# Block 2's shifts in two batches, its second pass's keys laid out early, the range verdict by a matmul, and two sets of norm statistics moved ahead

## The chip, the cores and the metric

The kernel runs on one NeuronCore of a Trainium2 chip. The metric is device time in microseconds, as the median of several runs. The profile is one execution, recorded by the hardware profiler. The engines are named PE (TensorE, matmuls and transposes), PEld (its weight loads), DVE (VectorE), ACT (ScalarE), POOL (GpSimd) and SP (SyncE, which here only issues DMAs). Each engine takes its instructions in the order in which they were written out for it, and waits on semaphores.

## The reference

Four blocks of a transformer are applied to `x`, 4 batches of 1024 tokens of width 288, with 16 heads of 18. Blocks 0 and 3 are attention over the tokens, attention over a context of 64, and a feed-forward part, all with 8-bit quantised linear layers. Block 1 is a context attention in two parts. Block 2, where most of the change lies, quantises queries, keys, values and probabilities with one scale for the whole tensor:

```python
        q = _fake_quant(q, NBITS)
        k = _fake_quant(k, NBITS)
        v = _fake_quant(v, NBITS)
        scale = 1.0 / np.sqrt(HD).astype(np.float32)
        scores = jnp.einsum('bhqd,bhkd->bhqk', q, k) * scale
        probs = jax.nn.softmax(scores, axis=-1)
        probs = _fake_quant(probs, SMBITS, always_zero=True)   # delta = max(probs) / 255
        out = jnp.einsum('bhqk,bhkd->bhqd', probs, v)
    ...
    n1 = _ln(h, ln1_g, ln1_b)
    h = h + _quant_attention(n1, n1, Wq1, Wk1, Wv1, Wo1, bo1)
    n2 = _ln(h, ln2_g, ln2_b)
    h = h + _quant_attention(n2, encoder_hidden_states, Wq2, Wk2, Wv2, Wo2, bo2)
    n3 = _ln(h, ln3_g, ln3_b)
    proj = n3 @ Wff1 + bff1
    a, gate = jnp.split(proj, 2, axis=-1)
    h = h + a * jax.nn.gelu(gate, approximate=False) @ Wff2 + bff2
```

The scale of the probabilities is the maximum over all batches, heads, queries and keys. So it is known only when every row of scores has been seen once.

## The kernel before

`x` stays in on-chip memory, as 32 tiles of 128 tokens (`NT` = 32, `NTB` = 8 tiles a batch). The blocks run one after the other: 0 and 1 together, then 2, then 3.

**Block 2, self-attention** (`fq_attn`, `fq_passes`). A first pass goes over all scores, four heads and 128 queries at a time: PE multiplies (line 3276), ACT takes the exponential and its row sum (line 2923), DVE the row maximum (line 2930). It leaves `top` and `sums`, 128 x 32 x 16 each: one column for each token tile and head, 512 in all. `prob_shift` (line 2382) turns them into the scale `pd` and a shift per row: reciprocal of the sums, a check of its range (`watch_range`), maximum over all partitions by an all-reduce on POOL, then Ln, Exp and a correction on ACT and DVE. The shift is split into three bfloat16 parts. `add_shift` (line 2405) lays a tile's three parts into the unused columns of a padded tile `spad` (POOL, line 2410), turns it with four transposes on PE (line 2416) and adds it to the queries (DVE, line 2417). With the shift in the queries, the exponential of the second pass gives the probability in steps of `pd`, which only has to be rounded.

The second pass (`attend_levels`, lines 3316 to 3328) goes over batch, half of the queries (4 tiles), head group and key tile. Its keys lie in `kz`, two buffers with zeros between the heads, cleared once by POOL (line 3023) and filled by four DMAs for each head group (`spread`, line 3031). The shifts of the next half, the output product and the queries of the context part are worked off beside it, one step per key tile (`aside`).

**Block 2's tail** (`fq_tail`) does context attention in the same manner (a first pass, `prob_shift`, then `probs` with `add_shift`) and the feed-forward part (`forward`), two generators woven together. Beside it `self_aside` prepares block 3's weights.

**Blocks 0 and 3.** `quant_self` does self-attention batch by batch and `levels(b)` starts with the norm statistics of batch `b` (`norm_stats`, line 1365, all on DVE). The context and feed-forward parts are generators (`ctx_stage`, `ff_stage`) which `run_stages` (line 1240) writes out in an order that a small planner finds: a generator yields what its last step costs on which engine, such as `"d8.5"` for 8.5 us of DVE, and may go on when that time is over.

**Order.** The program text gives each instruction's priority; the framework's scheduler works out the final order of each engine ahead of the run, and may draw an instruction forward past its place in the text when its inputs and its memory are there. Memory of a closed pool is given to later tiles, which then wait for the last use of what lay there.

**The verdict.** Each `watch_range` writes a column of `bad`. At the end `verdict` (line 1196) takes its maximum, over the columns on DVE and over the partitions by an all-reduce on POOL (line 1202); all engines load the result and branch: where a range was left, everything is computed again in a general way.

Of the kernel before, what the change touches and what calls it, by code (L numbers as in the profile page):

```python
# [21 lines left out]

# [33 lines left out]
class Net:  # L56
# [773 lines left out]
    def log_shift(self, pool, nm, sums, d, name):  # L830

        nc = self.nc
        n = sums.shape[1]
        y = pool.tile([P, n], F32, name=f"{name}y")
        nc.vector.tensor_scalar(y, sums, d, None, ALU.mult)
        z = pool.tile([P, n], F32, name=f"{name}z")
        nc.scalar.activation(z, y, AF.Ln)
        nc.vector.tensor_tensor(nm, nm, z, ALU.subtract)

        nc.scalar.activation(z, z, AF.Exp, scale=-1.0)  # L840
        nc.vector.tensor_tensor(z, z, y, ALU.mult)
        nc.vector.tensor_scalar(z, z, -1.0, 1.0, ALU.mult, ALU.add)
        nc.vector.tensor_tensor(nm, nm, z, ALU.add)
# [335 lines left out]
class Fast(Net):  # L1179
# [6 lines left out]
    def __init__(self, ctx, tc):  # L1186
        super().__init__(ctx, tc)
        self.bad = self.cp.tile([P, 96], F32, name="bad")
        self.n_bad = 0
        self.nmagic = self.cp.tile([P, 1], F32, name="nmagic")  # L1190
        self.nc.vector.memset(self.nmagic, -MAGIC)
        self.tiny = self.cp.tile([P, 1], F32, name="tiny")
        self.nc.vector.memset(self.tiny, 1e-8)
        self.nc.vector.memset(self.bad, 0.0)

    def verdict(self):

        nc = self.nc
        s = self.cp.tile([P, 1], F32, name="bads")
        nc.vector.tensor_reduce(s, self.bad, AX.X, ALU.max)  # L1200
        al = self.cp.tile([P, 1], F32, name="bada")
        nc.gpsimd.partition_all_reduce(al, s, P, bass_isa.ReduceOp.max)
        fl = self.cp.tile([1, 1], mybir.dt.int32, name="badi")
        nc.vector.tensor_copy(fl, al[0:1, :])
        return nc.values_load(fl[0:1, 0:1])
# [569 lines left out]
    def quant_self(self, L, w, beside, ready):  # L1775
# [5 lines left out]
        with ExitStack() as es:  # L1781
# [36 lines left out]
            def levels(b):  # L1818
# [5 lines left out]
                stats = self.norm_stats(b, 1e-6)  # L1824
# [169 lines left out]
            for b in range(B):  # L1994
                state[b]["a"] = at.tile([P, NTB, C], F32, tag="a", name="a")
                for g in range(NG):
                    if g + 1 < NG:
                        side.insert(0, operands(b, g + 1))
                    elif b + 1 < B:
                        while side:  # L2000
                            step()
                        side.append(operands(b + 1, 0))
                    if g == 1 and b + 1 < B:
# [145 lines left out]
    def ctx_stage(self, cw, g2, b2, pool, nb):  # L2149
# [15 lines left out]
        def tokens(b, hf):  # L2165
            t0 = b * NTB + hf * 4
            if hf == 0:
                stats[b] = self.norm_stats(b, 1e-5)
                there[b] = yield "d8.5", None, SIDE
# [212 lines left out]
    def prob_shift(self, gp, tp, top, sums, step):  # L2382


        nc = self.nc
# [5 lines left out]
        self.watch_range(self.R_MIN, self.R_MAX, r, "wr")  # L2391
        u = flat(top)
        nc.vector.tensor_tensor(r, r, u, ALU.mult)
        pd = self.prob_params(gp, r, "pd")
        nc.vector.memset(u, 0.0)
        self.log_shift(tp, u, flat(sums), pd, "ls")
        nc.vector.tensor_scalar(u, u, rstep, None, ALU.mult)
        parts = gp.tile([P, 3, NT * H], BF16, name="parts")
        for k in range(3):
            nc.vector.tensor_copy(parts[:, k, :], u)  # L2400
            if k < 2:
                nc.vector.tensor_tensor(u, u, parts[:, k, :], ALU.subtract)
        return pd, parts

    def add_shift(self, qT, sp, parts, t):


        nc = self.nc
        for k in range(3):
            nc.gpsimd.tensor_copy(  # L2410
                sp[:, :, D + k : D + k + 1], parts[:, k, t * H : (t + 1) * H].unsqueeze(2)
# [433 lines left out]
    def fq_passes(self, w, q, step, raw, rawq, qmx, qmn, side, aside):  # L2845

        tc, nc = self.tc, self.nc
        with ExitStack() as es:
# [8 lines left out]

            tops = ExitStack()
# [74 lines left out]
            with tops:  # L2933
                pd, parts = self.prob_shift(gp, tp, top, sums, step)
            es.enter_context(self.psum("f1o"))

# [3 lines left out]
            at, ot, ep = pool("f1o", 1), pool("f1q", 2), pool("f1p", 2)  # L2940
# [4 lines left out]
            spad = at.tile([P, H, HP], BF16, name="spad")  # L2945
            nc.gpsimd.memset(spad, 0.0)

            def shifts(b, hf):
                for j in range(hf * 4, hf * 4 + 4):
                    t = b * NTB + j  # L2950
                    self.add_shift(qk[:, b, 0, :, j * P : (j + 1) * P], spad, parts, t)
                    yield
# [68 lines left out]
            kzs = [at.tile([P, 2, S], BF16, name=f"kz{n}") for n in range(2)]  # L3021
            for kz in kzs:
                nc.gpsimd.memset(kz, 0.0)

            def spread(n):

                kz = kzs[n % 2]
                b, g = n // (2 * NG), n % NG
                for i in range(4):
                    rows = slice(i * HP, (i + 1) * HP)  # L3030
                    nc.sync.dma_start(kz[rows, i % 2, :], qk[rows, b, 1, g, :])

            spread(0)
            side.append(shifts(0, 0))
            while side:
                aside()
            late = []
            for b in range(B):
                for qh in range(2):
                    side[:0] = [shifts(*divmod(2 * b + qh + 1, 2))] if 2 * b + qh + 1 < 2 * B else []  # L3040
# [17 lines left out]
    def fq_tail(self, w, kq, keep, rawq, mx, nmn, beside):  # L3058
# [5 lines left out]
        with ExitStack() as es:  # L3064
# [6 lines left out]
            with (  # L3071
# [62 lines left out]
                pd, parts = self.prob_shift(gp, qp, top, sums, step)  # L3134
# [125 lines left out]
            for _ in spare:  # L3260
                pass
            self.weave([forward(before)], 1, 1)
# [178 lines left out]
```

## Time and profile before

| what | us |
|---|---|
| runs | 5096.9, 5111.57, 5107.95; median 5107.95 |
| the profiled execution | 5098.57 |
| its span, first to last instruction | 5096.9 |
| block 2, first pass (end of the scale's parameters to its last maximum) | about 1812 to 2414 |
| block 2, between the passes | 2414 to 2442 |
| block 2, second pass | 2442 to about 2990 |
| block 2, tail | from about 3004 |
| block 3, context and feed-forward parts | about 4640 to 5080 |

Over the whole span PE is busy 86%, ACT 61%, DVE 58% and POOL 26%; the granted clock of TensorE is 0.84 in the mean.

A line of the timeline gives start and duration in us, the engine (a q after it means its queue, which issues), the line of the code, the operation, what it writes and reads with the shape, how many instructions are merged, and in brackets how long the engine had been idle and which instruction ended that. A busy time by stretches gives the same for a stretch of time in one row.

### The profile page before, as it was taken

The numbers are of one execution on the slowest core, as the hardware profiler recorded it, in microseconds if no ns is written. First come the engines' busy times: TensorE is split into PE (matmuls) and PEld (weight loads), VectorE is DVE, ScalarE is ACT, GpSimd is POOL, SyncE is SP. The second block draws the span as 40 slices with busy tenths as digits, with TensorE's granted clock in tenths as the row PEclk, the third lists the DMA queues.
The fourth block names the chain that finished last, engine by engine and source line by source line (L and its number), as shares of the span: only waits on it lengthen the run. The fifth ranks groups of instructions, "written<-read, shape, count | busy, mean of one in ns | idle before, by whom it ended". The sixth has DMA issues, their size and how long they took to land. (4 is left out here: it accounts for less than half of the span.)

```text
span 5096.9 us, 63943 instructions
## 1 busy us (share of the span) xinstructions
PE 4360.7 (86%) x23291; PEld 1742.5 (34%) x23291; DVE 2961.5 (58%) x6542; ACT 3128.5 (61%) x4422; POOL 1348.8 (26%) x2109
## 2 busy tenths in 40 slices
PE   5999997889898979998788863899998999996686
PEld 2223322545565421100233332454542223322343
DVE  7343244665564679999687877433234334344775
ACT  3766765466663259998788853212216766764796
POOL 2110002442422566200122234111103110003664
PEclk9999998899899965555787875899998999997897
DMA  2000002100001221000000032000000000010000
GB/s 78 3 4 12 5 26 61 57 23 16 1 12 38 114 82 39 11 0 0 23 27 25 25 105 79 21 10 10 1 7 9 7 2 11 15 25 30 16 17 20
DMA packets 135637, 135.99 MB, mean 27 GB/s; under 512 B 69260, under 2 KB 111884, under 8 KB 133648
## 3 DMA queue, kind: packets, MB, share of 16 engines
q1 hardware_dynamic: 134112, 128.13, 8.4%
q0 software_dynamic: 1200, 3.69, 0.3%
q8 instruction: 185, 3.03, 0.2%
q14 instruction: 140, 1.15, 0.1%
HBM read 79.92 MB, written 43.47 MB: 24 GB/s over the span
## 5 line engine op out<-in xcount | busy, mean ns | idle before, releaser
L2021 ACT ACTIVATE e<-ps 128x1024 f32<-128x1024 f32 x1024 | 997.5, 1021 | 450.1 <-PE ps L2011 439.7
L2011 PE MATMUL ps<-qT,kT 32*128 32x512 f32 x4096 | 699.1, 658 | 1.8 <-ACT e L2021 1.8
L1971 PE MATMUL ps<-e,v 128*32 128x512 f32 x4096 | 564.1, 621 | 22.8 <-DVE oT L1982 21.1
L2930 DVE TENSOR_REDUCE top<-e 128x2 f32<-128x2048 f32 x256 | 561.9, 2275 | 18.5 <-ACT e L2923 18.5
L2923 ACT ACTIVATE e<-ps 128x1024 f32<-128x1024 f32 x512 | 534.0, 1369 | 19.7 <-PE ps L3276 11.3
L3325 ACT ACTIVATE e<-ps 128x1024 f32<-128x1024 f32 x512 | 484.0, 1056 | 84.3 <-PE ps L3316 67.3
L3276 PE MATMUL ps<-qk 32*128 32x512 bf16 x1024 | 511.1, 604 | 24.6 <-ACT e L2923 23.4
L1758 POOL TENSOR_TENSOR x<-x,y 128x288 f32<-128x288 f32 x192 | 153.1, 808 | 873.3 <-DVE y L1757 529.0
L1404 POOL TENSOR_TENSOR h<-h,g 128x288 f32<-128x288 f32 x224 | 179.5, 805 | 701.3 <-ACT h L1401 663.5
L3328 DVE TENSOR_SCALAR eb<-e 128x2048 bf16<-128x2048 f32 x256 | 322.0, 1261 | 48.6 <-ACT e L3325 46.1
L2923 ACT ACTIVATION_READ_ACCUMULATOR e<-ps 128x1 f32 x512 | 280.6, 550 | 0.0
L2011 PEld LDWEIGHTS ps<-qT,kT 32*128 32x128 f32 x4096 | 201.9, 187 | 226.0 <-issue 144.7
L3316 PE MATMUL ps<-qk,kz 64*128 64x512 bf16 x1024 | 225.0, 437 | 45.6 <-ACT e L3325 43.6
L2454 PE MATMUL psf<-hT,w 128*128 128x512 f32 x576 | 258.2, 600 | 0.6 <-ACT hT L2446 0.6
L1971 PEld LDWEIGHTS ps<-e,v 128*32 128x32 f32 x4096 | 81.9, 109 | 427.6 <-issue 353.6
L1349 PE MATMUL ps<-idb,q 128*128 128x128 bf16 (+2 forms) x1152 | 112.9, 243 | 124.5 <-ACT q L1333 70.8
L1401 ACT ACTIVATE h<-x,nmr,rstd 128x288 f32<-128x288 f32 x224 | 129.4, 623 | 137.7 <-DVE nmr L1393 69.7
L3276 PEld LDWEIGHTS <-qk 32*128 32x128 bf16 x1024 | 52.7, 99 | 465.4 <-issue 465.4
L3225 ACT ACTIVATE gl<-psf,bf 128x512 f32<-128x512 f32 x72 | 46.0, 684 | 268.5 <-PE psf L2458 264.2
L1354 ACT COPY qT<-ps 98x384 bf16<-98x384 bf16 (+3 forms) x256 | 151.6, 642 | 75.8 <-PE ps L1349 75.7
L1405 POOL TENSOR_TENSOR h<-h,b 128x288 f32<-128x288 f32 x224 | 180.4, 808 | 4.5
L277 PEld LDWEIGHTS <-qT 98*128 98x128 bf16 (+2 forms) x1344 | 135.7, 105 | 129.0 <-issue 43.9
(484 smaller groups left out, 7633.0 us busy)
## 6 DMA issues: line engine op xcount, KB each, us to landing
raw<-y SPq DMA_DIRECT2D x32, 432.0 KB
in<-raw SPq DMA_DIRECT2D x32, 432.0 KB
kz<-qk SPq DMA_DIRECT2D x128, 64.0 KB
wn<-in_L_wfc SPq DMA_DIRECT2D x12, 432.0 KB
x<-in_x SPq DMA_DIRECT2D x4, 1152.0 KB
vvo<-vt SPq DMA_DIRECT2D x16, 288.0 KB
vo<-vvo SPq DMA_DIRECT2D x4, 1152.0 KB
rawq<-y SPq DMA_DIRECT2D x32, 144.0 KB
```

Source lines behind the costliest of these rows:

```text
L1404: nc.gpsimd.tensor_tensor(h, h, g, ALU.mult)
L1405: nc.gpsimd.tensor_tensor(h, h, beta, ALU.add)
L1971: nc.tensor.matmul(acc[i * HP : (i + 1) * HP, :], lhsT=st["v"][:, kt, h * (D + 1) : h * (D + 1) + HP], rhs=es_[i // 2][:, i % 2, :], start ...
L2011: nc.tensor.matmul(pss[i // 2][:, i % 2, :], lhsT=self.row_tile(kT, i)[:, kt * P : (kt + 1) * P], rhs=self.row_tile(qT, i)[:, qh * 512 : ( ...
L2021: nc.scalar.activation(e, ps, AF.Exp, scale=SCALE)
L2454: nc.tensor.matmul(o, lhsT=lhs(i)[:, c, :], rhs=rhs(i)[:, c, :], start=(c == 0), stop=False)
L2923: nc.scalar.activation(e[:, j, :].rearrange("p (a n) -> p a n", a=2), sc, AF.Exp, scale=rstep, accum_out=sums[:, t, h0 + j : h0 + j + 1],)
L2930: nc.vector.tensor_reduce(top[:, t, h0 : h0 + 2], e, AX.X, ALU.max)
L3276: self.nc.tensor.matmul(ps[:, c, :], lhsT=self.row_tile(qT, i)[:, g, qt * P : (qt + 1) * P], rhs=self.row_tile(kT, i)[:, g, c * 512 : (c + ...
L3316: nc.tensor.matmul(pss[i][:, n, :], lhsT=kz[rows, i, kt * P : (kt + 1) * P], rhs=qT[rows, g, qh * 512 : (qh + 1) * 512], start=True, stop= ...
L3325: nc.scalar.activation(e[:, 2 * n : 2 * n + 2, :], ps, AF.Exp, scale=step)
L3328: nc.vector.tensor_scalar(eb, e, MAGIC, MAGIC, ALU.add, ALU.subtract)
```

## The change

- `prob_shift` takes the maximum straight after the product of reciprocal and `top`, and returns, beside the scale, two functions: one for the shifts of batch 0 (128 columns), one for the other three batches (384 columns), after which the range of `r` is watched. The parts lie in two tiles. The two functions share the scratch tiles `y` and `z`.
- In `fq_passes` the `kz` tiles are made and cleared before the first pass in the program's text, and the first `spread` is issued after the pass, ahead of `prob_shift`; so is the first `spad`. The shifts of batch 0's first half are added right after the first function; then the second function runs, and then come the loads of the second pass. A second `spad` serves the later halves.
- In `fq_tail` both functions run one after the other.
- `verdict` sums over the partitions by a product with ones on PE instead of the all-reduce.
- The statistics of batch 0 are written out earlier: those of the context part in the last batch of `quant_self`, and those of block 3's self-attention before the last `forward` of block 2. The planner's figure for the first is `"d0"`.

```diff
@@ verdict
-        al = self.cp.tile([P, 1], F32, name="bada")
-        nc.gpsimd.partition_all_reduce(al, s, P, bass_isa.ReduceOp.max)
         fl = self.cp.tile([1, 1], mybir.dt.int32, name="badi")
-        nc.vector.tensor_copy(fl, al[0:1, :])
+        with self.psum8("bad"):
+            ps = self.ps1()
+            nc.tensor.matmul(ps[0:1, 0:1], lhsT=s, rhs=self.ones[:, 0:1], start=True, stop=True)
+            nc.vector.tensor_copy(fl, ps[0:1, 0:1])
@@ quant_self
-                stats = self.norm_stats(b, 1e-6)
+                stats = self.early.pop("self", None) if b == 0 else None
+                if stats is None:
+                    stats = self.norm_stats(b, 1e-6)
...
+                    if (b, g) == (B - 1, 2):
+                        self.early["ctx"] = self.norm_stats(0, 1e-5)
@@ ctx_stage
-                stats[b] = self.norm_stats(b, 1e-5)
-                there[b] = yield "d8.5", None, SIDE
+                stats[b] = self.norm_stats(b, 1e-5) if b else self.early.pop("ctx")
+                there[b] = yield "d8.5" if b else "d0", None, SIDE
@@ prob_shift
-        self.watch_range(self.R_MIN, self.R_MAX, r, "wr")
-        u = flat(top)
-        nc.vector.tensor_tensor(r, r, u, ALU.mult)
-        pd = self.prob_params(gp, r, "pd")
-        nc.vector.memset(u, 0.0)
-        self.log_shift(tp, u, flat(sums), pd, "ls")
-        nc.vector.tensor_scalar(u, u, rstep, None, ALU.mult)
-        parts = gp.tile([P, 3, NT * H], BF16, name="parts")
-        for k in range(3):
-            nc.vector.tensor_copy(parts[:, k, :], u)
-            if k < 2:
-                nc.vector.tensor_tensor(u, u, parts[:, k, :], ALU.subtract)
-        return pd, parts
+        nc.vector.tensor_tensor(flat(top), r, flat(top), ALU.mult)
+        pd = self.prob_params(gp, flat(top), "pd")
+        parts = [gp.tile([P, 3, n * H], BF16, name=f"parts{n}") for n in (NTB, NT - NTB)]
+        yz = [tp.tile([P, (NT - NTB) * H], F32, name=f"ls{n}") for n in "yz"]
+
+        def shift(n):
+            tiles = slice(NTB, NT) if n else slice(0, NTB)
+            u = flat(top[:, tiles, :])
+            nc.vector.memset(u, 0.0)
+            self.log_shift_in(u, flat(sums[:, tiles, :]), pd, *(t[:, : u.shape[1]] for t in yz))
+            nc.vector.tensor_scalar(u, u, rstep, None, ALU.mult)
+            for k in range(3):
+                nc.vector.tensor_copy(parts[n][:, k, :], u)
+                if k < 2:
+                    nc.vector.tensor_tensor(u, u, parts[n][:, k, :], ALU.subtract)
+            if n:
+                self.watch_range(self.R_MIN, self.R_MAX, r, "wr")
+
+        return pd, parts, [partial(shift, n) for n in range(2)]
@@ fq_passes, before the first pass (kz and spread are taken from below)
+            at = pool("f1o", 1)
+            kzs = [at.tile([P, 2, S], BF16, name=f"kz{n}") for n in range(2)]
+            for kz in kzs:
+                nc.gpsimd.memset(kz, 0.0)
@@ fq_passes, after the first pass
-            with tops:
-                pd, parts = self.prob_shift(gp, tp, top, sums, step)
+            spread(0)
+            spad = tp.tile([P, H, HP], BF16, name="spad")
+            nc.gpsimd.memset(spad, 0.0)
+            pd, parts, shift = self.prob_shift(gp, tp, top, sums, step)
             es.enter_context(self.psum("f1o"))
...
+            shift[0]()
+            for _ in shifts(0, 0, spad):
+                pass
+            shift[1]()
+            tops.close()
...
-            spad = at.tile([P, H, HP], BF16, name="spad")
+            spad = at.tile([P, H, HP], BF16, name="spad2")
             nc.gpsimd.memset(spad, 0.0)
...
-            spread(0)
-            side.append(shifts(0, 0))
-            while side:
-                aside()
@@ fq_tail
-                pd, parts = self.prob_shift(gp, qp, top, sums, step)
+                pd, parts, shift = self.prob_shift(gp, qp, top, sums, step)
+                for f in shift:
+                    f()
...
+            self.early["self"] = self.norm_stats(0, 1e-6)
             self.weave([forward(before)], 1, 1)
```

`log_shift_in` is `log_shift` with its scratch tiles given by the caller, and `add_shift` takes a tile's columns from the first or the second parts tile.

## The prediction

> **What bounds the kernel now.** I first read busy time by stretches. In a row: from:to, length, busy time of PE, weight loads, DVE, ACT and POOL with their instruction counts, granted TensorE clock, DMA share, GB/s.
>
> ```profile
> 2414.00:2442.00 28.00, 2.94 (x20) 1.71 (x20) 15.37 (x28) 2.54 (x3) 8.76 (x22) 0.50 0.19 47
> 3135.00:3174.00 39.00, 2.99 (x19) 1.69 (x20) 21.33 (x69) 2.62 (x4) 6.80 (x22) 0.50 0.48 163
> 5075.00:5097.00 22.00, 3.64 (x27) 2.28 (x27) 2.28 (x6) 3.00 (x5) 2.07 (x4) 0.66 0.07 25
> ```
>
> Most of the span has a full engine (PE 86% in all), and the change touches none of that work. It touches three places where PE stands still: the hand-over between block 2's passes (28 us, PE busy 2.94), the same formula in block 2's tail, and the last 22 us. So I read those in order of time. The hand-over:
>
> ```profile
> 2413.99 3.34 DVE L2390 RECIPROCAL rs<-sums 128x512 f32<-128x512 f32 x1
> 2417.36 0.69 DVE L1218 TENSOR_REDUCE wr<-rs 128x1 f32<-128x512 f32 x1
> ...
> 2419.46 0.69 DVE L824 TENSOR_REDUCE pds<-rs 128x1 f32<-128x512 f32 x1
> ...
> 2420.28 0.38 POOL L826 PARTITION_ALL_REDUCE pdd<-pds  x1 [340.43 <-DVE pds L824]
> ...
> 2421.41 0.63 ACT L837 ACTIVATE lsz<-lsy 128x512 f32<-128x512 f32 x1 [12.50 <-DVE lsy L835]
> ...
> 2428.82 0.43 DVE L2400 CAST parts<-top 128x512 bf16<-128x512 f32 x1
> ...
> 2429.85 0.74 POOL L107 DMA_DIRECT2D g<-in_L_ln_g  x1 [9.18 <-DVE parts L2400]
> ...
> 2432.12 3.56 POOL L3023 MEMSET kz<- 128x2048 bf16 x2
> ...
> 2435.61 0.52 POOL L2410 COPY spad<-parts 128x16 bf16<-128x16 bf16 x3
> ...
> 2436.19 0.61 PE L2416 MATMUL ps<-idb,spad 128*128 128x128 bf16 x4 [30.55 <-POOL spad L2410]
> ...
> 2442.67 18.44 ACT L3325 ACTIVATE e<-ps 128x1024 f32<-128x1024 f32 x20 [18.69 <-PE ps L3316]
> ```
>
> One chain: DVE works out shifts for all 32 token tiles; POOL waits for its last cast (the loads' memory is still `top`'s), issues three loads, clears three tiles, and only then copies the shift into `spad`; PE turns it; four tiles later the second pass begins. The tail's chain has another end:
>
> ```profile
> 3152.30 0.38 SPq L2425 DMA_DIRECT2D w<-in_L_Wff  x1
> 3153.26 10.34 SPq L3149 DMA_DIRECT2D bf<-in_L_bff  x1
> 3163.77 13.89 SPq L3159 DMA_DIRECT2D qT<-qb  x3
> 3171.62 1.52 DVE L2417 TENSOR_TENSOR qT<-qT,ps 128x512 bf16<-128x512 bf16 x4 [16.33 <-DMA qT<-qb]
> ```
>
> Here SP's queue starts `w1` 0.14 us after the last cast (end 3152.16) has released `top`, sits 10.34 us in the next issue, then fetches `qT`, for which DVE waits. So the tail is set by when `top` is released, not by the first shift. The end:
>
> ```profile
> 5079.80 0.52 DVE L1755 SCALAR_TENSOR_TENSOR y<-ps,sc,wfc2sw 128x288 f32<-128x288 f32 x1 [2.36 <-PE ps L277]
> 5081.30 0.38 POOL L1202 PARTITION_ALL_REDUCE bada<-bads  x1 [6.13 <-DVE y L1755]
> 5089.25 1.53 POOL L1758 TENSOR_TENSOR x<-x,y 128x288 f32<-128x288 f32 x2 [7.57 <-issue]
> ```
>
> The check's all-reduce comes before the last two residual adds on POOL, and POOL then stands 7.57 us. Its queue shows two MODIFY_POOL_CONFIG at 5075.4 for the all-reduce and two at 5081.6 for the adds.
>
> **The change, part by part.**
>
> Hand-over. (a) The range check of `r` goes to the end of the second shift: the maximum `pds` follows the product directly, at 2418.05 instead of 2419.46: -1.4. (b) From the scale's start (2420.70) to the last cast's end (2429.25) are 8.55 us on 512 columns; now 128. The rows for 512 columns are 0.69 (two inputs), 0.43 to 0.49 (one), 0.63 (ACT); for 128x128 there are a one-input DVE row of 0.28 (L2336) and an ACT copy of 0.27 (L2497). Estimate from these: 0.28, 0.23 and 0.29. The scale, y, Ln, the 1.28 us table load, Exp and nine DVE steps with their 0.03 us gaps give 4.9: -3.65. (c) From last cast to first transposes are 6.94 us (2429.25 to 2436.19): three loads, 0.54 of `spad`, 3.56 of `kz`. Those memsets move ahead of the first pass's end, the loads behind the first shifts. What is left is one copy (0.25) and a hand-off (0.1): -6.6. The first copies after a pause took 0.93 at 3149.33; here that lies beside the next casts. Sum -11.65: the second pass starts near 2430.4 instead of 2442.0.
>
> What is put beside it: `spread(0)` issues four DMAs on SP; their source is ready at 1835 and SP is near idle until 2400, so they and 4.1 us of memset (POOL busy 196 of 602 us in the first pass) cost nothing; without that cover about 6. The second shift (384 columns) is about 5.2 us of DVE and two more table loads, and since it shares `y` and `z` with the first it ends near 2431 to 2433. Behind it, on POOL: the release of `top`, three loads, the memset of the new `spad`, the copies for tile 5; behind those, tile 5's transposes stand in PE's queue with score matmuls after them. That is what is late next. Bounds: 0 (DVE has 0.9 us free between adds, and tile 5 is needed 58 us later) and 6 (PE stands until 2436.3). I take 1.2, near the hidden end. Hand-over: **-10.5**.
>
> A rule to weigh: the Trainium skill, "GPSIMD Engine Reference", section "Instruction dispatch", says that the first call into freshly loaded code costs about 6 us. Against this change it would mean that copies right after the all-reduce (now ending at 2419.25) start at 2425.2 rather than 2423.1, so 1.2 us less gain. The row: copies ran from 2435.6, and the next MODIFY_POOL_CONFIG is at 2513.1, for a TENSOR_TENSOR (L2987). Copies, memsets and loads need no switch: I take no penalty. At the end of the program the rule gives 6 us where the row has 7.6 (5081.66 to 5089.25): removing it would be worth 8.0 by the rule, 9.6 by the row. I take the row.
>
> Tail. The check again leaves the front of the chain, but the all-reduce's code switch (3135.2, plus 5.9 as in 5075.4 to 5081.3) keeps it until 3141.1: only -0.7 of 1.4. Both shifts now run one after the other before `top` is free: 10.2 us from the scale against 8.55, by the same rates (first shift's z is free at 3.25, then Ln 0.5, table load 1.28, Exp 0.5, eight DVE steps). So +0.95, and some more for weight operations that slip into the gaps (1.4 us of them before). Bounds 0 and +3; taken **+1.2**.
>
> End. The all-reduce becomes a matmul of one column and a cast. POOL then adds the last `y` (ready 5080.32) by 5081.15, SP issues the store by 5081.5 instead of 5091.14, and the 5.76 us after it stay: **-9.6**. No row is a 1x1 matmul; the nearest (128x128 f32 transposes, 0.2 to 0.4) puts the verdict at about 5081.0 even if its bank waits for the last `y`: beside the add. Without that cover it costs under 1.
>
> Statistics.
>
> ```profile
> 3817.49 2.18 ACT L1401 ACTIVATE h<-x,nmr,rstd 128x288 f32<-128x288 f32 x4 [17.03 <-PE ps L3237]
> 4633.66 6.32 ACT L1401 ACTIVATE h<-x,nmr,rstd 128x288 f32<-128x288 f32 x12 [4.46 <-POOL x L1758]
> ```
>
> In block 3 both normalisations wait for memory that the part before releases. Batch 0's statistics are ready at 3731 and 4109 (in block 0 at 340), long before: the scheduler had already drawn them ahead. Price 0; if they were late, 7.6 us each (eight pairs of 0.45 and 0.17, thirteen small ones). The planner's first due time falls from 8.5 to 0, so its order may differ in the parts that it writes out. No row prices that; bounds -8.5 and +8.5, the shift itself; taken 0.
>
> Sum: -10.5 + 1.2 - 9.6 = **-18.9**. The profiled execution took 5098.57 (span 5096.9), so its like would take 5079.7. It lies 9.4 below the median 5107.95 of the runs shown; from the median the forecast is **5089.0**.
>
> **Rivals.** *The second shift is a new wait*: PE reaches tile 5 early and stands there; 6 us instead of 1.2, and the tail loses 3: 5095.6. For it: release, loads, memset and copies in one queue. Against: the order is made for when things are ready. *The planner gains*: before the first maximum of block 3's context part (4647.80) POOL runs ten multiplies and adds where eight would do; an order without the 8.5 us reservation gives up to 8.5: 5080.5. Against: all three first generators shift alike. *The check doesn't do what it says*: its bank or branch is late and the end keeps half: 5094, with a full second-shift wait 5099. *Slower*: the planner's order alone. Its place is the context and feed-forward parts (860 to 1430 and 4640 to 5075, some 1,000 us). It must cost 18.9 to cancel the rest and 34.2, or 3.4% of these parts, to make the kernel slower by the bound: 5123.3. For it: one order decides all the queues there; against: one due time of dozens moves.
>
> **How the numbers follow.** The runs before differ by 14.7 us, so 0.3% (15.3 us, limits 5092.6 and 5123.3) is about what can be told. Chances: forecast 0.60 (its own range 5081 to 5097), second-shift wait 0.15, planner gain 0.16, check late 0.05, slower 0.04. Faster: 0.82 of the first, a third of the second, 0.95 of the third, a fifth of the fourth: 0.70. Slower 0.04, else 0.26. The range reaches from the planner gain less half of the runs' spread (5074) to the late check with most of it (5105).
>
> **What would show it.** Right: L3325 starts about 16.5 us after the first pass's reciprocal, with a PE wait near 19 instead of 30.55; no L1202 all-reduce, and the last two L1758 adds directly after their `y`; `w1` issued 0.5 to 2 us later after the tail's last sums. Wrong: a PE wait on `spad` soon after the second pass starts, DVE or ACT still in the second shift when scores are there, or the parts that the planner orders longer or shorter by more than 3 us.

## The result, and the profile after

The changed kernel took 5085.69 us in the median of 5 runs (5075.41 to 5089.62), the kernel before 5106.36 beside it; the ratio is 0.9962, with a 95% interval of 0.9946 to 0.9978, that is 11 to 28 us less. A second set on another chip gave 0.9979 (0.9970 to 0.9987; median 5086.81). The kernel is faster by 0.2 to 0.4%, around the 0.3% that the prediction named as what can be told. The forecast was 5089.0 and a change of -18.9; by the ratios the sets gave -19 and -11, by the medians -20.7 and -13.3. The two profiled executions lie further apart: 5098.57 and 5075.41, with spans of 5096.9 and 5073.6.

First the busy time by stretches of the kernel after, with the columns of before: stretch, length, busy time of PE, weight loads, DVE, ACT and POOL, granted clock, DMA share, GB/s. The rows are the hand-over from reciprocal to first score, the tail from reciprocal to the first shift's addition, and the end.

```profile
2404.57:2423.40 18.83, 2.44 (x17) 1.41 (x17) 15.30 (x38) 5.51 (x7) 3.46 (x13) 0.50 0.00 0
...
3122.86:3160.92 38.06, 1.65 (x12) 1.22 (x13) 20.41 (x77) 5.51 (x7) 7.07 (x19) 0.50 0.50 166
5058.00:5075.00 17.00, 4.99 (x40) 3.26 (x38) 3.50 (x13) 3.71 (x7) 2.37 (x3) 0.70 0.10 32
```

The hand-over is 18.83 us long instead of 28.03 (2413.99 to 2442.02). DVE does as much as before in it; POOL's 8.76 us have become 3.46. The timeline of the kernel after, the hand-over and what follows it:

```profile
2404.57 3.34 DVE L2401 RECIPROCAL rs<-sums 128x512 f32<-128x512 f32 x1
...
2408.55 0.68 DVE L1223 TENSOR_REDUCE wr<-rs 128x1 f32<-128x512 f32 x1
2409.15 0.68 DVE L825 TENSOR_REDUCE pds<-top 128x1 f32<-128x512 f32 x1
...
2410.38 0.15 DVE L828 TENSOR_SCALAR pdd<-pdd 128x1 f32<-128x1 f32 x1
...
2414.58 0.25 POOL L2428 COPY spad<-parts 128x16 bf16<-128x16 bf16 x1 [4.24 <-DVE parts L2414]
...
2416.52 0.56 DVE L844 TENSOR_TENSOR lsz<-lsz,lsy 128x384 f32<-128x384 f32 x1 [0.48 <-ACT lsz L843]
2417.00 0.22 DVE L2414 CAST parts<-top 128x128 bf16<-128x128 f32 x1
...
2417.65 0.61 PE L2435 MATMUL ps<-idb,spad 128*128 128x128 bf16 x4 [21.69 <-POOL spad L2428]
...
2423.40 1.47 PE L3345 MATMUL ps<-qk,kz 64*128 64x512 bf16 x6 [0.61 <-DVE qk L2436]
2424.05 4.76 ACT L3354 ACTIVATE e<-ps 128x1024 f32<-128x1024 f32 x5 [7.56 <-PE ps L3345]
...
2425.11 0.74 POOL L108 DMA_DIRECT2D g<-in_L_ln_g  x1 [2.99 <-ACT e L3354]
...
2425.87 0.54 POOL L108 DMA_DIRECT2D b<-in_L_ln_b  x1
2426.02 1.67 DVE L3357 TENSOR_SCALAR eb<-e 128x2048 bf16<-128x2048 f32 x1 [1.51 <-ACT e L3354]
...
2427.79 0.54 POOL L2993 MEMSET spad<- 128x512 bf16 x1
...
2428.97 0.61 PE L2435 MATMUL ps<-idb,spad 128*128 128x128 bf16 x4 [2.32 <-POOL spad L2428]
2429.72 1.57 POOL L2428 COPY spad<-parts 128x16 bf16<-128x16 bf16 x3 [0.80 <-PE ps L2435]
2429.96 1.23 DVE L3357 TENSOR_SCALAR eb<-e 128x2048 bf16<-128x2048 f32 x1
2430.16 1.02 ACT L3354 ACTIVATE e<-ps 128x1024 f32<-128x1024 f32 x1 [1.36 <-PE ps L3345]
...
2431.35 0.61 PE L2435 MATMUL ps<-idb,spad 128*128 128x128 bf16 x4 [1.23 <-POOL spad L2428]
...
2433.09 13.16 ACT L3354 ACTIVATE e<-ps 128x1024 f32<-128x1024 f32 x14 [1.90 <-PE ps L3345]
```

Two things are to be seen. PE's long wait is 21.69 us instead of 30.55, and the loads and the memset now stand behind the first scores (2425.11 to 2428.33). But the operations of the second shift (the 384-column rows) stand between those of the first in DVE's queue: the third cast of the first batch (2417.00) is behind a 384-column product that itself waits for ACT. And once the second pass runs, PE stands twice for `spad`, which is the sign that the prediction named for a new wait. The start of the second pass in the kernel before, for comparison:

```profile
2441.48 0.60 PE L2416 MATMUL ps<-idb,spad 128*128 128x128 bf16 x4 [0.71 <-POOL spad L2410]
...
2442.22 0.52 POOL L2410 COPY spad<-parts 128x16 bf16<-128x16 bf16 x3 [0.80 <-PE ps L2416]
...
2442.67 27.73 ACT L3325 ACTIVATE e<-ps 128x1024 f32<-128x1024 f32 x30 [18.69 <-PE ps L3316]
...
2443.41 0.61 PE L2416 MATMUL ps<-idb,spad 128*128 128x128 bf16 x4
```

There the fifth tile was turned ahead of the first score (2441.48), PE turned the sixth without a wait (2443.41), and ACT ran 30 exponentials in a row; after, only four tiles stand ahead of the first score, and ACT ran five exponentials and stopped for 1.36 us and, one exponential later, for 1.90. The first 16 exponentials, from the start of the first to the start of the 17th, took 14.48 us before and 18.34 after.

The tail, the last cast on DVE and SP's queue in the timeline of the kernel after:

```profile
3140.78 0.34 DVE L2414 CAST parts<-top 128x384 bf16<-128x384 f32 x1
...
3141.28 0.38 SPq L2444 DMA_DIRECT2D w<-in_L_Wff  x1
...
3142.24 10.30 SPq L3176 DMA_DIRECT2D bf<-in_L_bff  x1
3152.79 14.16 SPq L3186 DMA_DIRECT2D qT<-qb  x3
3160.92 1.52 DVE L2436 TENSOR_TENSOR qT<-qT,ps 128x512 bf16<-128x512 bf16 x4 [16.62 <-DMA qT<-qb]
```

The chain is the one of before: `w1` goes out 0.16 us after the end of the last cast and 18.42 us after the reciprocal instead of 16.85. The end of the kernel after:

```profile
5064.55 0.52 DVE L1760 SCALAR_TENSOR_TENSOR y<-ps,sc,wfc2sw 128x288 f32<-128x288 f32 x1 [2.66 <-PE ps L278]
5065.12 0.19 PE L1208 MATMUL ps<-ones,bads 128*1 128x1 f32 x2 [0.68 <-DVE y L1760]
5065.14 0.79 POOL L1763 TENSOR_TENSOR x<-x,y 128x288 f32<-128x288 f32 x1 [2.38 <-DVE y L1760]
5065.41 0.15 DVE L1209 CAST badi<-ps 1x1 int32<-1x1 f32 x1 [0.35 <-PE ps L1208]
```

The last `y` is added 0.07 us after it is there; before it took 9.67 us. From the end of the last `y` to the end of the span are 8.54 us instead of 16.53.

Set out along the two profiled executions, the 23.2 us between the spans are: block 2 starts 9.4 us earlier already (time of its first pass's reciprocal); the hand-over to the first score gives 9.2; the second pass takes 6.5 more (3.9 of it in its first 16 exponentials; the pass took 548.4, 551.3 and 552.7 us in the three profiles with the hand-over of before, so some of it is chance); from the end of the second pass to the issue of `w1` 1.1 more; from there to block 3 (its first normalisation on ACT) 2.0 more; block 3's self-attention 5.1 less; the rest of block 3 1.1 less; the end 8.0 less. Block 3's self-attention took between 810.8 and 816.8 us in executions of all these kernels, 811.0 and 816.8 in two executions of the kernel after alone, so nothing is read from its share.

### The profile page after: what moved, and what is told of

Read it like the earlier page. It is cut to its first block, busy times and chain, and to the rows that moved or that the text cites. A ratio compares the mean times of both kernels' runs of the same rounds, so it can differ in the third digit from the quotient of the medians.

```text
span 5073.6 us, 63967 instructions
## 1 busy us (share of the span) xinstructions
PE 4363.8 (86%) x23293; PEld 1739.6 (34%) x23293; DVE 2978.9 (59%) x6566; ACT 3133.6 (62%) x4430; POOL 1350.6 (27%) x2109
## 5 line engine op out<-in xcount | busy, mean ns | idle before, releaser
L2956 ACT ACTIVATION_READ_ACCUMULATOR e<-ps 128x1 f32 x512 | 246.8, 483 | 0.0
L1359 ACT COPY qT<-ps 128x640 bf16<-128x640 bf16 (+3 forms) x256 | 152.9, 640 | 79.7 <-PE ps L1354 79.4
```

The lines of the kernel that those rows point to most:

```text
L2956: nc.scalar.activation(e[:, j, :].rearrange("p (a n) -> p a n", a=2), sc, AF.Exp, scale=rstep, accum_out=sums[:, t, h0 + j : h0 + j + 1],)
```

## The experiments

Times are compared with the kernel before on the same chip, and a gain in us is worked out from the ratio; where a stretch is named, it is from one profile of each kernel. Two stretches serve as gauges. Block 2's start is the issue of its first norm load on POOL, at 1629.18 before. The hand-over with what it gives back is the time from the first pass's reciprocal to the 33rd exponential of the second pass, 58.00 us before: it differs by less than 0.5 us between the executions of kernels that are alike there.

The theory after the result: three parts of the change act, each by itself, and the order that the planner writes out for blocks 0 and 1 is one of them. The first set takes the parts alone.

**The verdict alone** (`verdict_only`), on the kernel before:

```diff
-        al = self.cp.tile([P, 1], F32, name="bada")
-        nc.gpsimd.partition_all_reduce(al, s, P, bass_isa.ReduceOp.max)
...
-        nc.vector.tensor_copy(fl, al[0:1, :])
+            nc.tensor.matmul(ps[0:1, 0:1], lhsT=s, rhs=self.ones[:, 0:1], start=True, stop=True)
+            nc.vector.tensor_copy(fl, ps[0:1, 0:1])
```

> The kernel before with the verdict's product alone. Both theories: POOL's last two additions follow their y at once, the last store is issued 9.6 us earlier, and the end gains 8.0, because POOL's own branch and drain then come last. Ratio 0.9984 (8 us of 5106). If the gain of the end were given back elsewhere, under 3 us.

Measured: 5097.33 us, ratio 0.9996 (0.9986 to 1.0005), -2 us with an interval of -7 to +3. In its profile the end is 7.9 us shorter (8.65 instead of 16.53), as in the kernel after, and 6.6 us more are spread over the rest (2.2 up to the end of block 0's self-attention, 2.8 in the second pass, smaller pieces elsewhere), none of it near the change. The gain at the end is seen in the trace and hardly in the time, which misses the expected 8 us. The end itself is no chance of one execution: from the last `y` it took 15.7 to 16.5 us in the three profiles with the all-reduce at the end and 8.4 to 9.0 in the eleven without.

**The statistics alone** (`stats_only`), on the kernel before: the two early sets of statistics and the planner's figure.

```diff
-                stats[b] = self.norm_stats(b, 1e-5)
-                there[b] = yield "d8.5", None, SIDE
+                stats[b] = self.norm_stats(b, 1e-5) if b else self.early.pop("ctx")
+                there[b] = yield "d8.5" if b else "d0", None, SIDE
...
+                        self.early["ctx"] = self.norm_stats(0, 1e-5)
...
+            self.early["self"] = self.norm_stats(0, 1e-6)
```

> The kernel before with the early statistics and the due time d0 alone. Theory: the planner's order of blocks 0 and 1 is another one and gains about 10 us between 864 and 1620, as in the changed kernel's trace; 8 to 15 us in all (ratio 0.997 to 0.9985). Rival: these 10 us are differences between executions; then within 3 us of the kernel before.

Measured: 5092.70, ratio 0.9977 (0.9964 to 0.9990), -12 us (-18 to -5). Block 2 starts 10.1 us earlier. This part of the change, which the prediction priced at nothing, is the largest in the time.

**The hand-over alone** (`handover_only`), on the kernel before: `prob_shift` in two functions, keys and `spad` ahead, in `fq_passes` and `fq_tail`.

```diff
-            with tops:
-                pd, parts = self.prob_shift(gp, tp, top, sums, step)
+            spread(0)
+            spad = tp.tile([P, H, HP], BF16, name="spad")
+            nc.gpsimd.memset(spad, 0.0)
+            pd, parts, shift = self.prob_shift(gp, tp, top, sums, step)
...
+            shift[0]()
+            for _ in shifts(0, 0, spad):
+                pass
+            shift[1]()
+            tops.close()
```

> The kernel before with the shifts in two batches and the early keys alone. Theory: the second pass starts 9 to 10 us earlier after the first pass's reciprocal, 4 us are given back in its first eight key tiles and 1.5 in the tail: 3 to 5 us in all (ratio 0.999 to 0.9995). Rival: all of the hand-over is kept: 9 to 11 us (0.998).

Measured: 5098.50, ratio 0.9995 (0.9986 to 1.0004), -2.5 us (-7 to +2). Its profile has the same 18.82 us to the first score and the same 18.34 us for the first 16 exponentials as the kernel after; 53.03 us to the 33rd exponential against 58.00, so 5.0 us net. The rival that the 9 to 11 us come through is out. The three parts alone sum to -16.5 us, between the -19 and -11 of the whole change.

**The planner's figure kept** (`due_kept`), on the kernel after:

```diff
-                there[b] = yield "d8.5" if b else "d0", None, SIDE
+                there[b] = yield "d8.5", None, SIDE
```

> The changed kernel, but the planner still books 8.5 us for the first context statistics. Theory: blocks 0 and 1 lose their 10 us again, the rest stays: about 10 us slower than the changed kernel (5095). Rival: the early statistics themselves gain, or it is difference between executions: as the changed kernel (5086).

Measured: 5092.13, ratio 0.9987 (0.9981 to 0.9994), -7 us. The gain in blocks 0 and 1 is gone: block 2 starts at 1631.4, 2.2 us later than before, although the statistics are still written out early. So it is the figure, and the order that follows from it, and not the early statistics written out by themselves.

**Half the figure** (`due_half`), on the kernel after:

```diff
-                there[b] = yield "d8.5" if b else "d0", None, SIDE
+                there[b] = yield "d8.5" if b else "d4.25", None, SIDE
```

> The kernel after, but the first batch's statistics in the cross-attention part of blocks 0 and 1 keep half of their due time in the planner, d4.25, where the kernel after has d0 and the kernel before d8.5. Theory A, the planner's order is a different one for each figure and its worth is chance: the start of block 2 lies anywhere from 10 us below to 10 us above that of the kernel before (1629.2 us). Theory B, the gain follows the time that is no longer reserved: the start of block 2 lies about 5 us below (1624), half of the 9.3 to 10.1 that d0 gave, and the time about 5 us above the kernel after, 0.997 to 0.998 of the kernel before.

Measured: 5084.22, ratio 0.9972 (0.9961 to 0.9982). One row of busy time by stretches for each kernel shows what it does, from the end of block 0's self-attention to block 2's start. The kernel before:

```profile
864.15:1629.18 765.03, 648.90 (x3970) 410.39 (x3970) 437.44 (x1321) 430.36 (x725) 257.99 (x466) 0.90 0.09 27
```

The kernel after with the figure kept at 8.5:

```profile
863.75:1631.41 767.66, 648.99 (x3970) 409.12 (x3970) 437.91 (x1321) 430.69 (x725) 262.71 (x470) 0.89 0.09 27
```

The kernel after, with 0:

```profile
864.92:1619.88 754.96, 649.98 (x3970) 407.31 (x3970) 447.12 (x1321) 428.77 (x725) 262.08 (x471) 0.91 0.09 27
```

The kernel after with 4.25:

```profile
866.34:1620.97 754.63, 651.62 (x3970) 406.70 (x3970) 445.29 (x1321) 429.33 (x725) 262.67 (x470) 0.91 0.09 27
```

The work is the same, 3970 matmuls and 649 to 652 us of PE, in 765 to 768 us or in 755: what is saved is PE's idle time. And it is a step, not a slope: half of the figure gives all of the gain, which is against theory B, in which the gain follows the reserved time. Theory A, chance of the order, isn't excluded by one more order that lies within its bounds, but the order with 4.25 is nearly that with 0 (PE's order differs in six places with 47 of 3970 rows, where the order with 8.5 differs in some 3,900), so it is hardly a second draw. Why this order leaves PE less idle isn't shown. Over the ten profiled executions with 0 or 4.25 block 2 starts 7.3 to 14.8 us earlier than in the kernel before, over the three others with 8.5 it starts 2.0 to 2.7 later.

The second question is the hand-over: why 3.9 us come back at the start of the second pass. The theory: the second padded tile lies in memory that `top` releases and is cleared behind three loads, so the shifts of tiles 4 to 7 (counted from 0; the prediction's "tile 5" is tile 4) come late.

**The shifts later** (`shifts_later`), on the kernel after:

```diff
+                    if (b, qh) == (0, 0):
+                        side[:0] = [iter(range(8))]
```

> The kernel after, but the shifts of tiles 4 to 7, which the second pass has to make beside its first scores, start eight steps of the weave later, after GpSimd has done its three loads and its memset. My theory: the 3.8 us given back at the start of the second pass come from these shifts' copies standing behind GpSimd's 3.3 us of loads and memset, with TensorE held behind them. Then the first 16 exponentials take about 14.5 us as in the kernel before (18.3 in the kernel after) and the time is 3 to 4 us below the kernel after, 0.9955 of the kernel before. Rival: the copies are held by VectorE's rounding wherever they are put, and TensorE with them: then the loss moves to the second 16 exponentials and the first 32 together take as long as in the kernel after (33 us against 29 in the kernel before).

Measured: 5082.60, ratio 0.9971 (0.9961 to 0.9981). The first 16 exponentials took 17.24 us and the first 32 32.3 (33.6 in the kernel after, 29.3 before). Neither number of the expectation. Its timeline says why:

```profile
2427.54 0.54 POOL L2993 MEMSET spad<- 128x512 bf16 x1
...
2429.59 0.50 PE L2435 MATMUL ps<-idb,spad 128*128 128x128 bf16 x3 [1.49 <-POOL spad L2428]
...
2445.59 0.61 PE L2435 MATMUL ps<-idb,spad 128*128 128x128 bf16 x4
```

The framework's scheduler drew two of the four tiles forward again, to the same place behind the memset; only the other two moved, to 2445.59, where PE didn't wait for them. A step put later in the text of this program need not be later on the engine.

**The copies on VectorE** (`copies_dve`), on the kernel after:

```diff
-            nc.gpsimd.tensor_copy(
+            (eng or nc.gpsimd).tensor_copy(
...
-                    self.add_shift(qk[:, b, 0, :, j * P : (j + 1) * P], spad, parts, t)
+                    self.add_shift(qk[:, b, 0, :, j * P : (j + 1) * P], spad, parts, t,
+                                   self.nc.vector if (b, hf) == (0, 1) else None)
```

> The kernel after, but the three small copies of each of the tiles 4 to 7 are made by VectorE instead of GpSimd. They are behind neither GpSimd's loads nor its own waiting for VectorE. If GpSimd's queue and the stretched copies (1.57 us for three instead of 0.52, each time beside a rounding of 1.23 us on VectorE) make the loss, the first 16 exponentials take 14.5 to 15.5 us. If TensorE's own load is what makes it (four transposes in each of the first steps), they stay at 18 us or become longer, since VectorE's queue is then longer too.

Measured: 5078.10, ratio 0.9966 (0.9953 to 0.9979); the first 16 exponentials 17.26 us, again between the two. Its timeline:

```profile
2422.43 0.54 POOL L2994 MEMSET spad<- 128x512 bf16 x1
2423.01 0.36 DVE L2428 COPY spad<-parts 128x16 bf16<-128x16 bf16 x3 [0.68 <-POOL spad L2994]
2423.51 0.58 PE L2435 MATMUL ps<-idb,spad 128*128 128x128 bf16 x4 [1.31 <-DVE spad L2428]
...
2426.01 0.61 PE L2435 MATMUL ps<-idb,spad 128*128 128x128 bf16 x4 [0.53 <-DVE spad L2428]
```

The expectation was wrong in one point: on any engine the first copy has to wait for the tile's memset, and so for GpSimd's loads. It still takes the stretched copies away (0.35 us for three), and PE's second wait falls from 1.23 to 0.53.

**No such shifts at all** (`no_shift_47`), on the kernel after:

```diff
-                    side[:0] = [shifts(*divmod(2 * b + qh + 1, 2), spad)] if 2 * b + qh + 1 < 2 * B else []
+                    side[:0] = [shifts(*divmod(2 * b + qh + 1, 2), spad)] if 0 < 2 * b + qh and 2 * b + qh + 1 < 2 * B else []
```

> The kernel after, with the shifts of tiles 4 to 7 of the first batch left out altogether, so that 512 of the 2048 queries are attended without their shift; the loads, the memset and the release stay where they were. It gives the whole price of these shifts at this place. If they, and not the loads or the start itself, are the loss, the first 16 exponentials take 14.5 us or a little less. If 17 to 18 us stay, the loss is of another kind: ScalarE and VectorE start the pass with nothing ahead of them.

The queries without a shift are 512 of 4096, not of 2048. Measured: 14.60 us for the first 16 exponentials and 49.34 to the 33rd, against 18.34 and 53.03. The price of the four shifts at this place is 3.7 us, all of it theirs: loads, memset and release stood where they were. In the kernel before three such shifts stood beside the same scores, the fourth ahead of them, and cost nothing there (29.3 us from the first to the 33rd exponential, 29.9 here without any). Its time, 5083.07 and 0.9973 (0.9963 to 0.9982), tells it from the kernel after no more than the others do.

**One padded tile that stays** (`own_spad`), on the kernel after:

```diff
+            spad = at.tile([P, H, HP], BF16, name="spad")
-            for kz in kzs:
+            for kz in kzs + [spad]:
                 nc.gpsimd.memset(kz, 0.0)
...
-            spad = tp.tile([P, H, HP], BF16, name="spad")
-            nc.gpsimd.memset(spad, 0.0)
...
-            spad = at.tile([P, H, HP], BF16, name="spad2")
-            nc.gpsimd.memset(spad, 0.0)
```

> The kernel after, with one padded tile for the shifts from beginning to end: it lies beside the spread keys, in the pool that stays, so that the shifts of tiles 4 to 7 need no second padded tile, which lies in the released memory and is cleared behind the three loads. In the order that the scheduler wrote out, GpSimd now makes the copies of tiles 4 and 5 ahead of the loads, and those of 6 and 7 behind them. My theory: TensorE's wait of 2.3 us for the second padded tile, and the copies that then fall beside VectorE's roundings, are what costs 3.8 us. Then the first 16 exponentials take 14.5 to 15.5 us (18.3 in the kernel after), first score no later than 19 us after the reciprocal, and the time is 3 to 4 us below the kernel after in the same set. Rival: four shifts beside the first scores cost TensorE and ScalarE those 3 to 4 us wherever the copies stand; then 17 to 18 us as before.

Measured: 5082.21, ratio 0.9966 (0.9953 to 0.9979). The first score comes 19.66 us after the reciprocal (18.83 in the kernel after, no later than 19 expected), the first exponential after 20.31, and the first 16 take 16.28; to the 33rd they are 51.32, 1.7 us less than in the kernel after, against 3 to 4 expected. Its timeline:

```profile
2418.14 0.61 PE L2435 MATMUL ps<-idb,spad 128*128 128x128 bf16 x4 [0.90 <-POOL spad L2428]
...
2420.08 0.61 PE L2435 MATMUL ps<-idb,spad 128*128 128x128 bf16 x4
...
2421.30 1.23 DVE L3354 TENSOR_SCALAR eb<-e 128x2048 bf16<-128x2048 f32 x1 [0.16 <-ACT e L3351]
2421.41 1.25 POOL L108 DMA_DIRECT2D b<-in_L_ln_b  x1
...
2423.14 1.23 DVE L3354 TENSOR_SCALAR eb<-e 128x2048 bf16<-128x2048 f32 x1 [0.61 <-ACT e L3351]
2423.17 1.57 POOL L2428 COPY spad<-parts 128x16 bf16<-128x16 bf16 x3
2424.80 0.61 PE L2435 MATMUL ps<-idb,spad 128*128 128x128 bf16 x4 [1.40 <-POOL spad L2428]
```

Tile 4's transposes now stand before the first score (2418.14), which costs 0.8 us there, and tile 5's are made without a wait; the copies of tile 6 are behind the loads and fall beside a rounding, and PE waits 1.40 us. So with the wait for the second padded tile 1.7 us net are gone, and 2.0 of the 3.7 stay. Of these, 0.8 is tile 4's turn ahead of the first score, where the kernel before has it too; 1.2 are left beside the scores (31.01 us from the first to the 33rd exponential, 29.86 with no such shifts).

**One shift in the tail** (`one_shift_tail`), on the kernel after; `prob_shift` takes the places where its batches are cut, here one batch of all 32 tiles:

```diff
-                pd, parts, shift = self.prob_shift(gp, qp, top, sums, step)
+                pd, parts, shift = self.prob_shift(gp, qp, top, sums, step, (0, NT))
```

> The kernel after, but the tail's shift is made once over all 512 columns, as it was before the change; the first pass's hand-over keeps its two halves. My theory: the tail's doubled small operations are what made the stretch from its second reciprocal to the issue of w1 1.5 to 2.1 us longer in all three kernels that have them, so here it is back at 16.9 to 17.5 us (18.4 in the kernel after), and the time is 1.5 to 2 us below the kernel after, at 0.9958 of the kernel before, a gain too small for its interval. Rival: the stretch is longer because the range check or the pools' order moved; then it stays at 18.4 to 19 us.

Measured: 17.25 us from the reciprocal to the issue of `w1`. The nine profiles with two shifts in the tail have 18.4 to 19.8, the three with the tail of before 16.9 to 17.5. The doubled operations are the cause. In the time (5080.59; 0.9968, 0.9957 to 0.9979) it doesn't show by itself.

**The kernel after once more, and both repairs.** The program of after again (`after_again`), and `own_spad` with `one_shift_tail` (`own_spad_one_shift`), whose edits are those shown:

> The kernel after, once more, beside the variants of this set. At 0.996 to 0.997 of the kernel before if nothing but scatter stands between the sets. Its second pass must again take 18.3 us for its first 16 exponentials: that loss has come in every execution with this hand-over, and if it doesn't come here it is no property of the program.

> Both repairs together on the kernel after: one padded tile that stays, and the tail's shift made once over 512 columns. If each does what is expected of it alone, 3 to 4 us and 1.2 us, the time is 4 to 5 us below the kernel after in the same set, about 5078 us or 0.9955 of the kernel before; if only the tail's repair works, 1 us below it.

Measured: 0.9979 (0.9970 to 0.9987) for the kernel after, with 18.36 us for the first 16 exponentials; 5077.65 us and 0.9965 (0.9953 to 0.9977) for both repairs, with 51.33 us to the 33rd exponential and 17.25 us to `w1`, as in the single repairs. Its median is 9.2 us below that of the kernel after in the set, where 4 to 5 were expected; the two stretches account for 3.8 of it (53.04 to 51.33 and 19.32 to 17.25 us), the intervals overlap, and the rest isn't explained. It is the best version by the stretches that were repaired; the times alone don't prove it better.

## Why the prediction was right, and where it wasn't

The forecast of -18.9 us lies between the two sets' -20.7 and -13.3, but its terms do not: one was twice too large, one that was put at nothing was the largest, and they made up for each other. That the sum came out is in part luck.

**Hand-over, -10.5 predicted, -5.0 measured.** Of the pure gain of 11.65, 9.20 came. Step (a) gave 0.9 of 1.4: the scheduler still put one reduction of the range check (2408.55) ahead of `pds`. Step (b) gave 1.7 of 3.65: from the scale to the last cast's end are 6.84 us, not the 4.9 that the rates of 128 columns give, because DVE's queue holds the second shift's 384-column operations between the first's. The step that failed is the assumption that the second shift follows the first; the text has it so, the scheduler filled every gap of the chain with it. Step (c) gave 6.5 of 6.6, and the first copy took 0.25 us right after DVE's cast: no code load stood before it, so of the rule and the row the row was right there. From the first transposes to the first score 5.75 us passed, as before (5.83), but for four tiles instead of five: of what tile 4's turn no longer took there, slower copies and DVE's queue, busy with the second shift, used up nearly all.

The new wait, put at 1.2 within bounds of 0 and 6, was 4.2 us up to the 33rd exponential, in the main by the mechanism that the rival named: release, loads, memset and copies in one queue, with PE behind. The reason to go low was DVE's free time; what counted was that the tile's memset stands behind the release on POOL. Some 0.8 of the 4.2 is no wait but tile 4's turn, which before stood ahead of the first score. Beside the scores the four shifts cost 3.7 us (`no_shift_47`). With one padded tile that stays (`own_spad`) there is no wait for a second one, and tile 4 is turned ahead of the scores again: 2.5 of the 3.7 are gone from beside them, and 1.2 are left.

In the variants that leave the copies on POOL, PE's remaining waits come after copies that took 1.4 to 1.6 us for three beside a rounding of 1.23 us on DVE, where the kernel before has 0.5 to 0.7, begun ahead of a rounding or near its end. A rule of the Trainium skill that the prediction didn't weigh speaks of this: by "SBUF — State Buffer", section "SBUF: two separate sides", VectorE and GpSimd have one pair of ports in common, which some of VectorE's operations hold alone for their whole length. It agrees with the row: the copies end just after the rounding. One such hold, some 1.05 us (1.57 less 0.52), is about what `own_spad` has left. With the copies on DVE, where there is no such hold but still the wait for the memset, 1.6 us beside the scores were won. The two gains, 2.5 and 1.6, come to about the whole price, which fits two causes. No run took both away, so the holds' share is argued from these rows; no run separated it from the order of the transposes.

**Tail, +1.2 predicted, +1.6 to +2.9 measured** (18.4 to 19.8 us against 16.85 in the kernel before), within its bounds of 0 and 3 and by its mechanism, the release of `top`.

**End, -9.6 predicted, -8.0 measured.** The gap on POOL went entirely: the last store is issued 0.90 us after the last `y` instead of 10.49, 9.6 less. The step that failed is that what follows the store stays as it was: it was 6.04 us from the store's issue and is 7.64. The trace's records of branches and drains, which the views leave out, show where: before, GpSimd came to its branch on the verdict at 5082.44, within the 7.57 us for which its adds were held; now it comes to it at 5066.15, behind the last add, its next instruction follows at 5069.49, and its drain (2.11 us, from 5070.65) is the last work of the program, where SyncE's was before. The rule of the Trainium skill ("GPSIMD Engine Reference", "Instruction dispatch"), weighed in the prediction, would have given 8.0 and so the right figure, but by a wrong way: the pause that it prices at 6 us was 7.6 and is gone.

**Statistics, 0 predicted, about -10 measured.** The part about the statistics holds: they are ready early with or without the change, and `due_kept`, with early statistics and the old figure, gains nothing in blocks 0 and 1. The failed step is "bounds -8.5 and +8.5, taken 0" for the planner's order. It gave 9.4 us in the profiled pair, slightly outside, in blocks 0 and 1; between the means of all profiles, ten with 0 or 4.25 and four with 8.5, block 2's start lies 12.7 us apart. The rival that named a gain by the planner had the mechanism and the wrong place: block 3's parts took 432.5 and 431.2 us from the first maximum to the last `y`.

**The rest.** The terms as measured give -9.4 - 5.0 + 1.6 - 8.0 = -20.8 from the profiled pair, the sets of runs -11 to -21. That the end's 8 us hardly show in the time of `verdict_only` stays open.

## What to carry to other kernels

A figure that only feeds a planner is a change of the whole order after it: try two or three values and measure, since neither its sign nor its size can be read from the work that it stands for. When a long operation is cut in two so that a first part can go ahead, look in the order that comes out whether the second part was put between the operations of the first, and give what runs beside the new start its own memory, so that no release, load or memset stands before it. And at the end of a program, count every engine's way out, not only the one that was last so far.

## What the runs showed of the hardware that was not expected

GpSimd is held beside VectorE not only in its arithmetic: beside a rounding of 1.23 us three copies of 128x16 took 1.57 us instead of 0.52, and the issue of one load took 1.25 instead of 0.54, each ending just after the rounding. It goes the other way too: the first rounding of the second pass began 0.15 us after a load on GpSimd (2425.87 and 2426.02 above), ended 1.28 us after that load's issue and took 1.67 us; it took 1.66 or 1.67 in all nine profiles in which a load's issue of 0.54 us began so, and 1.23 in the five others. Not every operation holds GpSimd. From the hand-over of the kernel after:

```profile
2418.39 0.52 POOL L2428 COPY spad<-parts 128x16 bf16<-128x16 bf16 x3 [0.80 <-PE ps L2435]
2418.64 0.49 DVE L2412 TENSOR_SCALAR top<-top,rstep 128x384 f32<-128x384 f32 x1
...
2419.72 0.71 POOL L2428 COPY spad<-parts 128x16 bf16<-128x16 bf16 x3 [0.80 <-PE ps L2435]
2419.96 0.36 DVE L2414 CAST parts<-top 128x384 bf16<-128x384 f32 x1
```

Beside the scaling three copies took their 0.52 us, beside the shorter cast 0.71, and beside a subtraction of 0.55 us at 2421.46 they took 0.91.

The branch on the loaded verdict was dear at the end of this program: in the kernel after 3.3 us passed from GpSimd's branch to its next instruction, from TensorE's 4.3.

Executions of one program differ by up to 26 us (5088 to 5115 for the 101 runs of the kernel before beside the experiments), and part of it goes with TensorE's granted clock, which had means of 0.836 to 0.843 in them: a fit gives 1.7 us less for each 0.001 of the clock, with a correlation of -0.49. A change of 3 us in this kernel can therefore only be shown by the stretch in which it lies.
